# Four layers of a graph network on one core: where the adjacency transposes, the statistics and the additions of two layer boundaries stand in the order of work

## The chip, the cores and the metric

The kernel runs on one core of a Trainium2 chip. A core has five engines that run side by side, each with its own instruction stream: TensorE (PE in the profile) multiplies matrices and writes PSUM[...]; VectorE (DVE), ScalarE (ACT) and GpSimd (POOL) work element by element; SyncE (SP) here only issues the transfers between the chip's main memory and the core's SBUF. An engine takes its instructions in the order in which they stand in its stream. Engines wait for one another through semaphores, so an instruction whose input is late also holds up everything that stands behind it on its engine, whether or not that needed the late input.

The metric is the time of one execution on the device in microseconds (us). Of the kernel before there are three runs.

## The reference

The input x has 32 batches of 512 nodes with 128 features; adj is one 512 x 512 matrix with about one entry in eight above zero. There are four layers, each of the same outer form: normalise every node's features, cut at zero, apply a graph layer, add to x. Cut to what matters here:

```python
# each layer i:  h = max(layernorm(x), 0);  x = x + layer_i(h)

# layer 0: an attention matrix from adj's pattern and a list e of 256 values
m = adj > 0
idx = cumsum(m.reshape(-1)) - 1            # number of each entry above zero
A = softmax(where(m, e[0][idx], -9e15), axis=1)
out = (A * I) @ (h @ W[0]) + (A * (1 - I)) @ (h @ W[1]) + bias

# layer 1: two rounds of hops along adj, for A1 = A2 = adj
x1 = einsum('bnf,nw->bwf', h, adj)
x2 = 2 * einsum('bnf,nw->bwf', x1, adj) - h
out = relu(concat(h, x1, x2, x1, x2) @ Theta1 + bias)

# layer 2: weights adj * adj
features = relu(h @ psi_w + psi_b)
messages = einsum('nm,bnd->bmd', adj * adj, features)
out = relu(concat(messages, h) @ phi1_w + phi1_b) @ phi2_w + phi2_b

# layer 3: scores of h with itself, exp(8 tanh(s / 8)) times adj, divided by the row's sum
```

Because e has only 256 entries, the first 256 entries of adj above zero have a value of their own and all later ones share the last. The kernel finds the row and column of each of those 256 with counts and comparisons, and places their values in A by products of matrices that hold a single one in each row.

## The kernel before: what the change touches

The batches are taken in 16 groups q of two, and the groups in 8 pairs r. A product with the 512 x 512 matrix is done block by block with seven products in place of eight (Winograd's form of Strassen's scheme). GpSimd forms the differences of the right operand, named rt_g (layer 0), rt_h and rt_w (layer 1) and rt_feat (layer 2). The seven products are numbered by k; they use three PSUM banks a, c and d, which are written again as soon as VectorE or ScalarE has read them:

```python
    ORDER = ((1, "a", True), (6, "c", True), (5, "d", True), (7, "c", False), (2, "a", False),
             (4, "c", False), (3, "d", False))

    def products(name, form, left, right, evict):

        banks = {}
        for k, g, first in ORDER:
            if first:
                banks[g] = bank(f"p_{name}_{g}")
            form(banks[g], left[k], right[k], first)
            evict(k, banks[g])
            yield
```

```python
# layer 1 and layer 2 evict with this one: bank c holds k = 6, then 7, then 4
        def evict(k, p):
            p = p[:, :H]
            if k == 1:
                nc.scalar.copy(m1[0], p)
            elif k == 6:
                nc.vector.tensor_add(m1[1], p, m1[0])
            elif k == 7:
                nc.vector.tensor_add(m1[2], p, m1[0])
            ...
```

The preparation of layer 0 counts the entries of adj above zero (rc, incl, before), finds the 256 places (of_row, row_of, col_of, at_row, at_col, at_part) and fills att:

```python
    of_row = prep.tile([P, NT, NE], BF16, name="of_row")
    pb = bank("p_before")
    pg = [bank(f"p_row_{kk}") for kk in range(NK)]
    for t in range(NT):
        s = prep.tile([P, NE], F16, tag="lt", name=f"lt_{t}", bufs=4)
        nc.gpsimd.tensor_scalar(s, cols[:, :NE], incl[:, t : t + 1], None, OP.is_lt)
        nc.vector.scalar_tensor_tensor(of_row[:, t, :], cols[:, :NE], before[:, t : t + 1], s,
                                       OP.is_ge, OP.mult)
        for kk in range(NK):
            nc.tensor.matmul(pg[kk], of_row[:, t, blk(kk)], m[:, t, :], start=(t == 0), stop=(t == NT - 1))
    for kk in range(NK):
        for t in range(NT):
            nc.tensor.matmul(pb[:, kk : kk + 1], of_row[:, t, blk(kk)], befh[:, t : t + 1],
                             start=(t == 0), stop=(t == NT - 1))
# ... (parts of e in three lower-precision pieces, on GpSimd)
    us = [prep.tile([P, N], F32, tag="u", name=f"u_{t}", bufs=NT) for t in range(NT)]

    def entries(t):
        nc.scalar.mul(us[t], m[:, t, :], elastn)
        nc.gpsimd.tensor_add(att[:, t, :], us[t], att[:, t, :])

    entries(0)
    pt = [bank(f"p_adjT_{j}") for j in range(NT)]
    for t in range(NT):
        transpose_rows(pt, adj_s, t)
    for j in range(NT):
        nc.scalar.copy(adjT[:, j, :], pt[j])
    adjT_d = bounce.tile([N, N], F32, tag="adjT", name="adjT_d", bufs=1)
    nc.sync.dma_start(adjT_d.rearrange("(t p) w -> p t w", p=P), adjT)
    for kk in range(NK):
        s = prep.tile([P, N], F16, tag="scr", name=f"scr_r{kk}", bufs=2)
        nc.vector.tensor_scalar(s, pc, rows[:, kk : kk + 1], None, OP.is_le, OP.add,
                                accum_out=row_of[:, kk : kk + 1])
    ln = [stats_steps(q, powers=q < 2) for q in range(4)]
    go(ln[0])
    entries(1)
    go(ln[1])
# ... (scans, at_row, at_col, at_part, the first groups' h and its transposes)
    p = bank("p_qk_t")
    nc.tensor.transpose(p[:, blk(0)], qw, ident)
    nc.tensor.transpose(p[:, blk(1)], kw, ident)
    qkT = prep.tile([P, 2, D], F32, name="qkT")
    nc.scalar.copy(qkT, tiles(p)[:, :2, :])
    go(normal[1], 4)
    entries(2)
    entries(3)
    go(normal[1])
    bias(0)
```

`transpose_rows` makes the transpose of adj, which is written to main memory and read again much later, for layer 3:

```python
    def transpose_rows(banks, src, t):

        for j in range(NT):
            nc.tensor.transpose(banks[j][:, blk(t)], src[:, t, blk(j)], ident)
```

Up to the last pair but one of layer 0 the order on TensorE, VectorE, ScalarE and GpSimd is the order of the source. After that point a scheduler orders the instructions by its own estimates of their times:

```python
    for r in range(NQ // 2 - 1):
        round0(r)
    by_source.__exit__(None, None, None)

    next_layer = layer1(0)
    next(next_layer)
    waiting = [[next_layer, layer0_last()], [layer1(1)]]
    for r in range(2, NQ // 2):
        waiting += [[], [layer1(r)]]
    waiting[5].append(square())
    waiting[-1].append(layer2(0))
    waiting += [[layer2(q)] for q in range(1, NQ)]
    waiting += [[layer3(q)] for q in range(NQ)]
    active = []
    while waiting or active:
        if waiting:
            active += waiting.pop(0)
        if not waiting and len(active) == 2:
            active.reverse()
        active = [g for g in active if next(g, active) is not active]
```

Every generator in `active` is advanced one step in each turn of the loop; `yield` ends a step. The last pair of layer 0 and layer 1 before:

```python
    def layer0_last():
        round0(NQ // 2 - 1)
        go(own[NQ - 2])
        go(own[NQ - 1])
        yield

    # in layer1(r), the steps before this one: h[A] | turned(A), h[C] | first(A), turned(C) |
    # first(C), weighed(A) | weighed(C), right2 |
        for _ in products(f"l1_{r}", by_token, sums["adj"], right2, evict):
            pass
        p = bank(f"p_l1_{r}_e")
        own(p, 1, 1, True)
        done(p, u[2], 1, 1)
        if C == NQ - 1:
            yield
            yield
        ln_stats(A)
        ln_stats(C)
```

`turned` transposes h on VectorE (hb), sends it through main memory to get it feature by feature (hT), and forms rt_h; `first` forms x1T with `mixed`; `weighed` multiplies by Theta1 (p_w) and copies the result to w on ScalarE; the products named p_l then give the layer's output. `ln_stats` computes mean and variance of the new x with BATCH_NORM_STATS2 (bn), then the scale rs and the shift sh. In layer 0, `add` adds a partial sum to a block of x on GpSimd (line 751), and lines 745, 748 and 833 add products to the same blocks on VectorE. Layer 2 before:

```python
        feat = []
        for b in range(2):
            pf = projected(f"p_feat_{q}_{b}", (at(hT, b), psi))
            feat.append(late.tile([P, NT, D], F32, tag="hs", name=f"feat_{q}_{b}", bufs=6))
            nc.vector.tensor_add(feat[b], pf, spread(psib, NT))
            nc.scalar.activation(feat[b], feat[b], AF.Relu)
        yield
        right = right_blocks(lambda J, b: feat[b][:, 2 * J : 2 * J + 2, :], f"feat_{q}", [nc.gpsimd] * 4)
        if q % 2 == 0:
            msgs.append(quad_tile(f"msgT_{q}"))
        msgT = msgs[-1][:, q % 2, : 2 * N].rearrange("p (b w) -> p b w", b=2)
        for _ in mixed(f"msgT_{q}", sums["sq"], right, msgT):
            pass
        for b in range(2):
            for i in range(0, NT, 2):
                xi = xt[q][:, b, i : i + 2, :]
                tc.keep_in_program_order(nc.gpsimd.tensor_add(xi, xi, spread(phi2b, 2)))
        yield
```

## Time and profile before

| What | Before |
|---|---|
| median of three runs | 987.52 us (986.81 to 988.62) |
| span of the profiled execution | 989.5 us |
| instructions in it | 15113 |
| mean granted TensorE clock | 0.991 |
| ScalarE, first h of layer 0 | 19.25 us |
| TensorE, first product of layer 0 (p_l_a) | 39.12 us |
| TensorE, first product of layer 1 (p_x1T_a) | 192.96 us |
| TensorE, first product of layer 2 (p_msgT_a) | 467.90 us |
| main memory read and written | 44.17 MB and 40.89 MB |

The profile's page gives for one execution the time for which each engine was busy, the same in 40 equal slices of the span (a 9 means 90% or more), the groups of instructions that cost most, and the chain of work that ended last. Further views answer about a stretch of time: which instructions ran, how long an engine sat idle before one, and what released it (written as [idle <- releaser]). The granted clock is the share of its full rate at which TensorE was allowed to run; at 0.50 every product takes twice as long. A product is written as its output, then the inputs: `p_l_c<-rt_w,adj_s`.

### The profile page before, as it was taken

Reading aid. Unit: us, or ns where it says so; the run is one execution under the profiler, and the core shown is the slowest. Engines: PE = TensorE matmul, PEld = TensorE weight load, DVE = VectorE, ACT = ScalarE, POOL = GpSimd, SP = SyncE. Lnnn points to the kernel's source line nnn. Section 1 sums busy time; section 2 is a strip of 40 time slices with the busy share of each in tenths; the row PEclk is TensorE's granted clock in tenths of the full one; section 3 lists DMA queues with packets and bytes.
Section 4 is the critical chain, followed back from the end, with each engine's and each line's share of the span. In section 5 each row is a group of like instructions: output and inputs, shape, how many; then the busy total and the mean of one; then the engine's idle time right before and its main releaser. Section 6 shows DMA issues by size and latency. Waiting matters only on the chain.

```text
span 989.5 us, 15113 instructions
## 1 busy us (share of the span) xinstructions
PE 960.1 (97%) x5449; PEld 783.5 (79%) x5450; DVE 582.9 (59%) x1312; ACT 473.9 (48%) x1058; POOL 439.6 (44%) x482
## 2 busy tenths in 40 slices
PE   4999999899999999999799999999999999999998
PEld 2799999788988989889677777777667776777776
DVE  7778896636456445646367655656564444454444
ACT  4874555042332242376437454544665554445553
POOL 6686997923463532530623334444133322233322
PEclk9999999999999999999899999999999999999999
DMA  9145645223311311444133432232132121121111
GB/s 255 50 128 153 187 121 141 82 66 119 115 43 43 85 45 47 123 107 107 43 98 105 118 86 79 71 86 85 44 86 75 54 64 65 51 77 44 54 32 43
DMA packets 82330, 86.04 MB, mean 87 GB/s; under 512 B 6737, under 2 KB 72529, under 8 KB 82257
## 3 DMA queue, kind: packets, MB, share of 16 engines
q1 hardware_dynamic: 82256, 85.09, 30.7%
q8 instruction: 43, 0.70, 0.3%
q14 instruction: 31, 0.25, 0.1%
HBM read 44.17 MB, written 40.89 MB: 86 GB/s over the span
## 4 chain that ended last, share of the span: by engine, by line
PE 84%; POOL 6%; DVE 6%; ACT 2%; issue 1%; DMA 1%; SPq 0%; DVEq 0%; POOLq 0%; ACTq 0%
PE p_av L1025 12%; PE p_score L1010 11%; PE p_l_c L356 7%; PE p_w L405 5%; PE p_msgT_c L349 5%; PE p_l_a L356 5%; PE p_l_d L356 5%; PE p_x1T_c L349 4%; PE p_hv L405 3%; PE p_msgT_d L349 3%; PE p_feat L405 3%; PE p_qkh L997 3%; PE p_l L405 3%; PE p_msgT_a L349 3%; PE p_phi L980 3%; PE p_phi L981 3%
## 5 line engine op out<-in xcount | busy, mean ns | idle before, releaser
L231 ACT ACTIVATE h<-x,sh,rs 128x128 f32<-128x128 f32 x512 | 209.9, 484 | 81.9 <-PE p_x1T_d L349 33.2
L1015 POOL TENSOR_TENSOR ex<-ex,adjTx 128x512 f32<-128x512 f32 x64 | 83.1, 1300 | 206.4 <-ACT ex L1013 206.4
L1011 ACT ACTIVATE ex<-p_score 128x512 f32<-128x512 f32 x128 | 71.9, 587 | 124.6 <-issue 113.0
L1025 PEld LDWEIGHTS p_av<-qkh_hv,ex 128*128 128x128 f32 x1024 | 118.4, 191 | 9.4 <-issue 7.4
L1025 PE MATMUL p_av<-qkh_hv,ex 128*128 128x129 f32 x1024 | 120.1, 275 | 0.8 <-POOL ex L1015 0.8
L1010 PE MATMUL p_score<-qkh_hv,hT 128*128 128x512 f32 x256 | 115.2, 593 | 0.0
L265 DVE STREAM_TRANSPOSE hb_hT<-h 128x512 f32<-128x512 f32 x120 | 81.9, 697 | 35.6 <-ACT h L231 34.1
L1015 DVE TENSOR_TENSOR ex<-ex,adjTx 128x512 f32<-128x512 f32 x64 | 45.4, 709 | 82.2 <-ACT ex L1013 82.1
L203 DVE BATCH_NORM_STATS2 bn<-x 128x6 f32<-128x256 f32 x256 | 93.0, 418 | 1.1
L1010 PEld LDWEIGHTS p_score<-qkh_hv,hT 128*128 128x128 f32 x256 | 46.2, 190 | 46.5 <-issue 44.7
L1013 ACT ACTIVATE ex<-ex 128x512 f32<-128x512 f32 x128 | 76.6, 630 | 1.9
L330 POOL TENSOR_TENSOR rt_w<-w 128x512 f32<-128x512 f32 x16 | 20.3, 1269 | 108.2 <-ACT w L872 108.2
L330 POOL TENSOR_TENSOR rt_feat<-feat,feat 128x256 f32<-128x256 f32 x16 | 11.6, 728 | 127.3 <-ACT feat L964 127.3
L370 ACT COPY x1T<-p_x1T_a 128x256 f32<-128x256 f32 x16 | 5.9, 370 | 94.0 <-PE p_x1T_a L349 94.0
L405 PE MATMUL p_w<-th,x1T 128*128 128x128 f32 x256 | 49.5, 275 | 0.0
L405 PE MATMUL p_w<-th,hs 128*128 128x128 f32 x256 | 49.5, 275 | 0.0
L405 PEld LDWEIGHTS p_hv<-vw,hT 128*128 128x128 f32 x256 | 33.6, 192 | 15.3 <-issue 8.1
L975 POOL TENSOR_TENSOR x<-x,phi2b 128x256 f32<-128x256 f32 x64 | 44.5, 726 | 0.0
L982 ACT ACTIVATE msgT<-p_phi,phi1b 128x512 f32<-128x512 f32 x32 | 21.7, 678 | 41.0 <-PE p_phi L981 41.0
L405 PEld LDWEIGHTS p_w<-th,hs 128*128 128x128 f32 x256 | 40.1, 192 | 0.8
L964 ACT ACTIVATE feat<-feat 128x512 f32<-128x512 f32 x32 | 20.1, 629 | 42.2 <-DVE feat L963 42.2
L651 POOL TENSOR_TENSOR hd<-hT,adiag 128x512 f32<-128x512 f32 x32 | 39.8, 1272 | 1.2 <-ACT adiag L764 1.2
(229 smaller groups left out, 2085.3 us busy)
## 6 DMA issues: line engine op xcount, KB each, us to landing
d_hT<-hb_hT SPq DMA_DIRECT2D x240, 128.0 KB
hT<-d_hT SPq DMA_DIRECT2D x60, 512.0 KB
x<-in_x_dram SPq DMA_DIRECT2D x32, 256.0 KB
out_dram<-x SPq DMA_DIRECT2D x31, 256.0 KB
adj_s<-in_adj_dram SPq DMA_DIRECT2D x4, 256.0 KB
adjT_d<-adjT SPq DMA_DIRECT2D x1, 1024.0 KB
sq<-in_adj_dram SPq DMA_DIRECT2D x4, 256.0 KB
adjTx<-adjT_d SPq DMA_DIRECT2D x4, 256.0 KB
```

The source lines that it names most:

```text
L203: nc.vector.bn_stats(st[:, k].rearrange("p e s -> p (e s)"), xt[q][:, b, t : t + 2, :].rearrange("p t f -> p f t"))
L231: nc.scalar.activation(h[:, b, t, :], xt[q][:, b, t, :], AF.Relu, bias=shift[q][:, i : i + 1], scale=scale[q][:, i : i + 1])
L265: nc.vector.transpose(hb[:, :, b].rearrange("p j t r -> p t j r"), h[:, b].rearrange("p t (j c) -> p t j c", c=QR))
L349: nc.tensor.matmul(p[:, :H], b[:, k, :], a[:, k, :], start=(first and k == 0), stop=(k == 1), skip_group_check=True)
L356: nc.tensor.matmul(p[:, i * 2 * D : (i + 1) * 2 * D], a[:, k, blk(i)], b[:, k], start=(first and i == 0 and k == 0), stop=(k == 1), skip_g ...
L405: nc.tensor.matmul(p[:, blk(t)], hT(t), w, start=(i == 0), stop=(i == len(terms) - 1))
L975: tc.keep_in_program_order(nc.gpsimd.tensor_add(xi, xi, spread(phi2b, 2)))
L1010: nc.tensor.matmul(ps, hT[:, t, b, :], qkh, start=True, stop=True)
L1011: nc.scalar.activation(ex[:, t, :], ps, AF.Tanh, scale=1.0 / (8.0 * math.sqrt(D)))
L1013: nc.scalar.activation(ex[:, t, :], ex[:, t, :], AF.Exp, scale=8.0)
L1015: eng.tensor_mul(ex[:, t, :], ex[:, t, :], adjTx[0][:, t, :])
L1025: nc.tensor.matmul(po[:, i, : D + 1], ex[:, t, blk(i0 + i)], hv[:, t, :], start=(t == 0), stop=(t == NT - 1))
```

## The change

It is a change of order, save for 24 added products whose result nobody reads.

- The 16 transposes of adj and the four copies of their results stand right behind the load of adj, ahead of the counts. They stood behind the counts.
- `keep_busy(n)` issues n products of 128 x 512 into a bank that is not read, six after the counts and eighteen after p_before. They are meant to keep TensorE from standing still.
- The four comparisons lt go from GpSimd to VectorE; elastn, u and the additions to att are placed differently among the first statistics.
- The last pair of layer 0 is put into the part that keeps the order of the source, with the first two steps of layer 1 woven in by hand; layer 1's second pair starts one turn earlier; the statistics of groups 14 and 15 come a turn later.
- In layer 1 a `yield` stands between the last addition and the statistics, so these belong to the next turn.
- In layer 2 the differences rt_feat are formed in the same turn as feat, not in the next.

```diff
--- before.py
+++ after.py
@@ -461,6 +461,20 @@
     att = square_tile("att")
     for t in range(NT):
         nc.gpsimd.tensor_scalar(att[:, t, :], m[:, t, :], -1.0, -NEG, OP.add, OP.mult)
+    pt = [bank(f"p_adjT_{j}") for j in range(NT)]
+    for t in range(NT):
+        transpose_rows(pt, adj_s, t)
+    for j in range(NT):
+        nc.scalar.copy(adjT[:, j, :], pt[j])
+    adjT_d = bounce.tile([N, N], F32, tag="adjT", name="adjT_d", bufs=1)
+    nc.sync.dma_start(adjT_d.rearrange("(t p) w -> p t w", p=P), adjT)
+
+    def keep_busy(n):
+
+        p = bank("p_idle")
+        for _ in range(n):
+            nc.tensor.matmul(p, upto[:, 0, blk(0)], upto[:, 0, :], start=True, stop=True)
+
 
     pi = bank("p_incl")
     for t in range(NT):
@@ -477,13 +491,14 @@
     nc.vector.tensor_sub(before, incl, rc)
     befh = prep.tile([P, NT], BF16, name="befh")
     nc.vector.tensor_scalar(befh, before, float(NE), None, OP.min)
+    keep_busy(6)
 
     of_row = prep.tile([P, NT, NE], BF16, name="of_row")
     pb = bank("p_before")
     pg = [bank(f"p_row_{kk}") for kk in range(NK)]
     for t in range(NT):
-        s = prep.tile([P, NE], F16, tag="lt", name=f"lt_{t}", bufs=4)
-        nc.gpsimd.tensor_scalar(s, cols[:, :NE], incl[:, t : t + 1], None, OP.is_lt)
+        s = prep.tile([P, NE], F16, tag="lt", name=f"lt_{t}", bufs=2)
+        nc.vector.tensor_scalar(s, cols[:, :NE], incl[:, t : t + 1], None, OP.is_lt)
         nc.vector.scalar_tensor_tensor(of_row[:, t, :], cols[:, :NE], before[:, t : t + 1], s,
                                        OP.is_ge, OP.mult)
         for kk in range(NK):
@@ -492,13 +507,12 @@
         for t in range(NT):
             nc.tensor.matmul(pb[:, kk : kk + 1], of_row[:, t, blk(kk)], befh[:, t : t + 1],
                              start=(t == 0), stop=(t == NT - 1))
+    keep_busy(18)
     row_of = prep.tile([P, NK], F32, name="row_of")
     col_of = prep.tile([P, NK], F32, name="col_of")
     at_row = prep.tile([P, NK, N], BF16, name="at_row")
     at_col = prep.tile([P, NK, N], BF16, name="at_col")
     at_part = prep.tile([P, 3, NK, N], BF16, name="at_part")
-    elastn = prep.tile([P, 1], F32, name="elastn")
-    nc.gpsimd.tensor_scalar(elastn, elast, -1.0, None, OP.mult)
 
     ecoln = prep.tile([P, NK], F32, name="ecoln")
     nc.gpsimd.tensor_scalar(ecoln, ecol, -1.0, None, OP.mult)
@@ -512,26 +526,25 @@
         if i < 2:
             nc.gpsimd.tensor_sub(ecoln, ecoln, part)
         parts.append(part)
+    elastn = prep.tile([P, 1], F32, name="elastn")
+    nc.gpsimd.tensor_scalar(elastn, elast, -1.0, None, OP.mult)
     us = [prep.tile([P, N], F32, tag="u", name=f"u_{t}", bufs=NT) for t in range(NT)]
 
+    def value(t):
+        nc.scalar.mul(us[t], m[:, t, :], elastn)
+
     def entries(t):
-        nc.scalar.mul(us[t], m[:, t, :], elastn)
         nc.gpsimd.tensor_add(att[:, t, :], us[t], att[:, t, :])
 
-    entries(0)
-    pt = [bank(f"p_adjT_{j}") for j in range(NT)]
-    for t in range(NT):
-        transpose_rows(pt, adj_s, t)
-    for j in range(NT):
-        nc.scalar.copy(adjT[:, j, :], pt[j])
-    adjT_d = bounce.tile([N, N], F32, tag="adjT", name="adjT_d", bufs=1)
-    nc.sync.dma_start(adjT_d.rearrange("(t p) w -> p t w", p=P), adjT)
+    value(0)
+    value(1)
     for kk in range(NK):
         s = prep.tile([P, N], F16, tag="scr", name=f"scr_r{kk}", bufs=2)
         nc.vector.tensor_scalar(s, pc, rows[:, kk : kk + 1], None, OP.is_le, OP.add,
                                 accum_out=row_of[:, kk : kk + 1])
     ln = [stats_steps(q, powers=q < 2) for q in range(4)]
     go(ln[0])
+    entries(0)
     entries(1)
     go(ln[1])
     bk = prep.tile([P, NK], F32, name="bk")
@@ -557,7 +570,9 @@
     nc.tensor.transpose(p[:, blk(1)], kw, ident)
     qkT = prep.tile([P, 2, D], F32, name="qkT")
     nc.scalar.copy(qkT, tiles(p)[:, :2, :])
-    go(normal[1], 4)
+    go(normal[1], 2)
+    value(2)
+    value(3)
     entries(2)
     entries(3)
     go(normal[1])
@@ -812,6 +827,8 @@
                 go(own_a)
             elif i == 3:
                 add(1, 1, 2)
+                if not more:
+                    next(next_layer)
                 if C + 4 < NQ:
                     normalise(C + 4)
                 if r >= 3:
@@ -838,11 +855,11 @@
         if r + NQ // 4 < NQ // 2:
             loads(r + NQ // 4)
 
-    def layer0_last():
-        round0(NQ // 2 - 1)
+    def layer0_stats():
+
+        yield
         go(own[NQ - 2])
         go(own[NQ - 1])
-        yield
 
     x1 = []
 
@@ -935,6 +952,7 @@
         p = bank(f"p_l1_{r}_e")
         own(p, 1, 1, True)
         done(p, u[2], 1, 1)
+        yield
         if C == NQ - 1:
             yield
             yield
@@ -962,8 +980,8 @@
             feat.append(late.tile([P, NT, D], F32, tag="hs", name=f"feat_{q}_{b}", bufs=6))
             nc.vector.tensor_add(feat[b], pf, spread(psib, NT))
             nc.scalar.activation(feat[b], feat[b], AF.Relu)
-        yield
         right = right_blocks(lambda J, b: feat[b][:, 2 * J : 2 * J + 2, :], f"feat_{q}", [nc.gpsimd] * 4)
+        yield
         if q % 2 == 0:
             msgs.append(quad_tile(f"msgT_{q}"))
         msgT = msgs[-1][:, q % 2, : 2 * N].rearrange("p (b w) -> p b w", b=2)
@@ -1049,13 +1067,13 @@
             nc.gpsimd.tensor_copy(sq[:, i, :], s)
         yield from sum_steps(sq, "sq")
 
-    for r in range(NQ // 2 - 1):
+    next_layer = layer1(0)
+    for r in range(NQ // 2):
+        if r == NQ // 2 - 1:
+            next(next_layer)
         round0(r)
     by_source.__exit__(None, None, None)
-
-    next_layer = layer1(0)
-    next(next_layer)
-    waiting = [[next_layer, layer0_last()], [layer1(1)]]
+    waiting = [[next_layer, layer1(1), layer0_stats()]]
     for r in range(2, NQ // 2):
         waiting += [[], [layer1(r)]]
     waiting[5].append(square())
```

How the instructions stand after it, engine by engine, is known from the two built programs. On TensorE layer 1's p_w products, which stood between the x1T products of the pair ahead, now stand behind all seven of them. On VectorE the first x1T eviction of a pair (line 372) stands ahead of three of the four last statistics, and was behind them. On GpSimd at the first boundary the order was hd, rt_h, hs and the additions to x in turns, and is now four hd, three additions, twelve rt_h. At the second boundary it was rt_w, then rt_feat, and is now rt_feat, then rt_w.

More of the change, by code (lines that the diff above doesn't have):

```diff
@@ L964, in layer2 @@
             nc.scalar.activation(feat[b], feat[b], AF.Relu)
+        right = right_blocks(lambda J, b: feat[b][:, 2 * J : 2 * J + 2, :], f"feat_{q}", [nc.gpsimd] * 4)
         yield
-        right = right_blocks(lambda J, b: feat[b][:, 2 * J : 2 * J + 2, :], f"feat_{q}", [nc.gpsimd] * 4)
         if q % 2 == 0:
```

## The prediction

> **What bounds the kernel now.** I read first the page's busy times and the slices, to see whether one engine carries the span.
>
> ```profile
> PE 960.1 (97%) x5449; PEld 783.5 (79%) x5450; DVE 582.9 (59%) x1312; ACT 473.9 (48%) x1058; POOL 439.6 (44%) x482
> PE   4999999899999999999799999999999999999998
> ```
>
> TensorE (PE) is busy for 960.1 of 989.5 us, and its work does not get less. So a change that only reorders can win two things: the 29.4 us in which PE stands still, and the time in which it works at half clock. The slices that are not 9 (first, eighth, twentieth, last) say where to look. Next I read the waits of PE, summed by what it waited for (us in total, times, longest).
>
> ```profile
> PE p_incl L468 <- DVE rch L458: 8.3, 1, 8.3
> PE p_msgT_c L349 <- POOL rt_feat L330: 5.4, 1, 5.4
> PE p_x1T_c L349 <- DVE rs L217: 5.0, 7, 2.6
> PE p_hT L249 <- ACT h L231: 3.6, 1, 3.6
> ```
>
> The first is the load of adj and the first row counts, which nothing in the diff shortens. The other three are the change's three targets: layer 1 to layer 2 (5.4), layer 0 to layer 1 and inside layer 1 (5.0 in seven pieces), and the preparation (3.6). Then the stretches of 1 us around them (columns: PE, PEld, DVE, ACT, POOL busy; then the granted clock, DMA share, GB/s):
>
> ```profile
> 26.00:27.00 1.00, 1.00 (x3) 0.30 (x2) 0.16 (x1) 1.00 (x4) 0.91 (x1) 0.50 1.02 367
> 200.00:201.00 1.00, 1.00 (x4) 0.73 (x4) 0.59 (x2) 0.00 (x0) 0.00 (x0) 0.50 0.00 0
> 480.00:481.00 1.00, 1.00 (x3) 0.74 (x3) 0.00 (x0) 0.00 (x0) 0.00 (x0) 0.50 0.00 0
> ```
>
> PE is full there, but at clock 0.50. Finer stretches put the half clock at 20.6 to 27.4, 198.1 to 201.5 and 474.6 to 481.4 us: each follows a gap. A gap thus costs twice. Last I read the order in time at the two layer boundaries:
>
> ```profile
> 189.25 0.73 POOL L330 TENSOR_TENSOR rt_h<-h 128x256 f32<-128x256 f32 x1
> 194.83 1.26 POOL L751 TENSOR_TENSOR x<-x,u_l 128x512 f32<-128x512 f32 x1
> 196.13 0.69 DVE L833 TENSOR_TENSOR x<-p_l_e,x 128x512 f32<-128x512 f32 x1 [2.62 <-POOL x L751]
> 197.74 0.41 DVE L372 TENSOR_TENSOR x1T<-p_x1T_c,x1T 128x256 f32<-128x256 f32 x1
> 198.29 2.05 PE L349 MATMUL p_x1T_c<-adj_s,rt_h 128*128 128x256 f32 x4 [2.57 <-DVE rs L217]
> ...
> 468.99 1.27 POOL L330 TENSOR_TENSOR rt_w<-w 128x512 f32<-128x512 f32 x1 [18.57 <-ACT w L872]
> 474.01 0.72 POOL L330 TENSOR_TENSOR rt_feat<-feat,feat 128x256 f32<-128x256 f32 x1
> 476.15 2.08 PE L349 MATMUL p_msgT_c<-sums_sq,rt_feat 128*128 128x256 f32 x4 [5.41 <-POOL rt_feat L330]
> 484.93 1.89 PE L356 MATMUL p_l_a<-w,adj_s 128*128 128x256 f32 x8
> ```
>
> At 190 us GpSimd works on layer 1's differences (rt_h) while layer 0's last addition to x waits behind them. VectorE stands in order at that x (2.62 us), and behind it lies the eviction L372 that frees PE's bank. At 469 us GpSimd takes four rt_w first; rt_feat, which PE needs next, had its input at 466.0 us and starts at 474.0.
>
> [...] half clock lasted 6.8, 3.4 and 6.8 us, once after a gap of only 2.57 us. [...] of_row took 0.70, 0.69, 0.69 us beside GpSimd's lt and 0.48 us after it.
>
> **The change, part by part.** Times are on the clock of before, each part alone.
>
> *Preparation.* The 16 transposes of adj leave 14.2 to 16.2 us and run as adj arrives; their four ScalarE copies (2.05 us) leave 15.9 to 17.9. The four lt (3.65 us on GpSimd, 9.0 to 12.7) go to VectorE, at about 0.2 us each (a 128x512 comparison of the same types takes 0.35). Four pairs of lt and of_row at some 0.7 us end at 12.2 instead of 13.1. The first statistics then end near 15.0, and GpSimd, free of lt and of the att addition (1.27 us) that stood ahead, ends scale and shift near 17.6 instead of 19.2. ScalarE's first h starts 1.6 us earlier. The second pair's scale and shift gain less, because both att additions (2.5 us) now stand ahead: near 22.7 instead of 23.3. ScalarE then does two h, two u, six h, and reaches its first exponential near 27.3 instead of 28.06. The unread products (6, then 18, at 0.215 us each at full clock: 1.3 and 3.9 us) fill PE's idle time; none is waited for, except that a cold PE makes the first six last 2.6 us and could delay p_row, whose reader VectorE comes only near 16.4. If they keep the clock, the 32 products of p_first and p_val run at 1.72 us a row from the start, and the 1.4 us (0.91, 0.20, 0.29) that ScalarE lost in waits for least shrink. ScalarE's row of exponentials, scalings, g copies and table load then sets the start of layer 0: 0.75 plus about 1.0 gives 1.8 us.
>
> *Layer 0 to layer 1.* GpSimd's order now is hd, the three additions, then rt_h. The rt_g end at 179.2, four hd at 1.27 at 184.2, the additions near 188.0 (the third waits for L739). L833 follows p_l_e at 192.6, no longer 196.1. VectorE then still has some 1.5 us of statistics ahead of L372, so that runs near 195.3 to 196.2, and PE, which has x1T_d done at 195.0, waits 0.6 to 1.3 us[...]. Before, these seven x1T products took from 192.96 to 203.4, 10.4 us; at 0.86 us each they need 6.05. Of the 4.4 us and the 0.31 before p_l_c, about 3.5 are won.
>
> *Inside layer 1.* Six gaps remain (5.0 less 2.6: 2.4 us; one of 0.78, five near 0.3). The order on VectorE now puts L372 ahead of three of the statistics (1.1 us). But PE has also lost the p_w products that stood between, so c7 waits 0.15 us where it waited 0.3. I count 1.2 us.
>
> *Layer 1 to layer 2.* rt_feat is now ahead of rt_w on GpSimd, and PE does all seven msgT products in a row. rt_feat can start at 466.1, its third operation, which c needs, ends near 468.2; PE is at 468.8. The rt_w follow, 469.0 to 474.1, and p_l_c needs the second of them at 477.5. PE from msgT_a (467.90) to p_l_a (484.93) took 17.0 us; its work is 7 x 0.86 + 16 x 0.112 = 7.8. That gives 9.2; I count 9.0.
>
> Sum: 1.8 + 3.5 + 1.2 + 9.0 = 15.5, and 987.5 - 15.5 = 972.0 us. Layer 3 and the last 3.7 us of idle PE are untouched.
>
> **Rivals.** *Preparation goes cold or slower.* For it: the h transposes come one in 0.39 us, and PE was at half clock through just such a stretch; then rows take 3.4 us for a while. This leaves 0 to 1 us of the 1.8: 973 to 974. [...] *VectorE becomes the bound at the first boundary.* It now carries the transposes hb of two pairs and all statistics between 185 and 196 with GpSimd beside it; an L218 there took 0.91 us instead of 0.2. L372 at 197.5 would make the gap 2.5 us and cold again: 975. *The second boundary only moves its wait.* ScalarE was full from 458 to 474 us with h of layer 2, and the copies of w and msgT stand between them; if L370 slips by 2 us, PE waits that long: 974. Against: its place is the same as before. *Everything is found*: preparation follows PE rather than ScalarE (3.0), the boundary gives 4.4, layer 1 2.4, then 968.5, still short of 967.8, which 2% would need.
>
> **Range and chances.** Most of the sum rests on the last part, whose arithmetic leaves little room. The parts before may each miss by 1 us, and a new gap with its cold clock costs 3 to 5. I give 967.5 to 978. Faster by over 2% needs 19.8 us, all parts at their limit: 0.07. Slower by over 2%: 0.01.
>
> **What would show it.** PE's waits should no longer list rt_feat, the longest p_x1T_c wait should be under 1.5 us, and p_hT's under 1.5. Half clock should be gone near 196 and 475. L833 should not wait for POOL. PE's busy time should grow by about 5 us of unread products. A page with rt_feat's wait still there, or a new row above 2 us, makes the prediction wrong; so does layer 0 starting later than 39 us.

## Result, and the profile after

The changed kernel takes 974.49 us (median of 4 runs, 973.98 to 974.86) where the kernel before, run beside it, took 988.07: a ratio of 0.9859, 95% interval 0.9837 to 0.988. Run again beside the kernel before, it gave 974.23 and 0.9854 (0.9837 to 0.987). That is 1.4% less, within 2%; 972.0 had been predicted, with a range of 967.5 to 978.

The page of the changed kernel, busy times and slices:

```profile
PE 959.0 (99%) x5474; PEld 781.9 (80%) x5474; DVE 581.0 (60%) x1316; ACT 474.6 (49%) x1058; POOL 436.5 (45%) x478
PE   7999999999999999999999999999999999999998
PEclk9999999999999999999999999999999999999999
```

TensorE's idle time fell from 29.4 to 13.7 us. The dents in the eighth and twentieth slice are gone, only the first and last are left. Its waits (us in total, times, longest):

```profile
PE p_adjT L444 <- DMA adj_s<-in_adj_dram: 4.7, 2, 3.8
PE p_x1T_c L349 <- DVE x1T L372: 2.5, 7, 0.4
PE p_msgT_c L349 <- DVE msgT L372: 0.6, 1, 0.6
```

rt_feat (5.4 us) and the transposes of h (3.6) no longer stand in the list, and p_x1T_c's longest wait went from 2.6 to 0.4. The stretches of 1 us that answer to the three shown of before (last columns: granted clock, DMA share, GB/s):

```profile
26.00:27.00 1.00, 1.00 (x6) 0.49 (x5) 0.63 (x2) 1.00 (x4) 1.00 (x2) 1.00 0.98 365
194.00:195.00 1.00, 1.00 (x5) 0.90 (x6) 1.00 (x3) 0.00 (x0) 1.00 (x3) 1.00 0.04 13
463.00:464.00 1.00, 1.00 (x6) 0.80 (x5) 0.19 (x1) 1.00 (x4) 0.92 (x2) 1.00 0.00 0
```

TensorE is as full as before, but at clock 1.00, and starts five or six products in a us where it started three or four. The order in time at the two boundaries:

```profile
182.64 3.76 POOL L766 TENSOR_TENSOR x<-x,u_l 128x512 f32<-128x512 f32 x3
191.28 0.69 DVE L850 TENSOR_TENSOR x<-p_l_e,x 128x512 f32<-128x512 f32 x1
193.43 0.40 DVE L372 TENSOR_TENSOR x1T<-p_x1T_c,x1T 128x256 f32<-128x256 f32 x1
193.98 1.10 PE L349 MATMUL p_x1T_c<-adj_s,rt_h 128*128 128x256 f32 x4 [0.22 <-DVE x1T L372]
...
458.92 0.73 POOL L330 TENSOR_TENSOR rt_feat<-feat,feat 128x256 f32<-128x256 f32 x1 [15.47 <-ACT feat L982]
461.63 1.03 PE L349 MATMUL p_msgT_c<-sums_sq,rt_feat 128*128 128x256 f32 x4
461.79 1.27 POOL L330 TENSOR_TENSOR rt_w<-w 128x512 f32<-128x512 f32 x1
468.60 1.89 PE L356 MATMUL p_l_a<-w,adj_s 128*128 128x256 f32 x8
```

GpSimd's three additions to x are done at 186.4, before layer 1's differences; VectorE's last addition (L850, L833 before) waits for nothing; TensorE waits 0.22 us for L372, not 2.57 (the list of before put these waits down to L217, which ran just behind L372). Below, rt_feat comes before rt_w, and TensorE goes from p_msgT_a (460.76) to p_l_a (468.60) in 7.8 us, not 17.0.

### The profile page after: what moved, and what is told of

It reads as the page before. It is cut to its first block, busy times and chain, and to the rows that moved or that the text cites. A ratio compares the mean times of both kernels' runs of the same rounds, so it can differ in the third digit from the quotient of the medians.

```text
span 972.7 us, 15180 instructions
## 1 busy us (share of the span) xinstructions
PE 959.0 (99%) x5474; PEld 781.9 (80%) x5474; DVE 581.0 (60%) x1316; ACT 474.6 (49%) x1058; POOL 436.5 (45%) x478
## 4 chain that ended last, share of the span: by engine, by line
PE 91%; DVE 4%; ACT 2%; DMA 2%; SPq 1%; issue 0%; POOL 0%; DVEq 0%; ACTq 0%
PE p_av L1043 12%; PE p_score L1028 11%; PE p_l_c L356 9%; PE p_l_a L356 6%; PE p_l_d L356 6%; PE p_w L405 5%; PE p_msgT_c L349 4%; PE p_x1T_c L349 4%; PE p_feat L405 3%; PE p_hv L405 3%; PE p_msgT_d L349 3%; PE p_msgT_a L349 3%; PE p_qkh L1015 3%; PE p_l L405 3%; PE p_g L405 3%; PE p_phi L998 3%
## 5 line engine op out<-in xcount | busy, mean ns | idle before, releaser
L265 DVE STREAM_TRANSPOSE hb_hT<-h 128x512 f32<-128x512 f32 x120 | 81.7, 697 | 33.4 <-ACT h L231 33.1
L370 ACT COPY x1T<-p_x1T_a 128x256 f32<-128x256 f32 x16 | 5.9, 370 | 84.3 <-PE p_x1T_a L349 84.3
L1048 DVE SCALAR_TENSOR_TENSOR x<-p_av,rsum,x 128x128 f32<-128x128 f32 x128 | 39.1, 347 | 1.9
```

The lines of the kernel that those rows point to most:

```text
L265: nc.vector.transpose(hb[:, :, b].rearrange("p j t r -> p t j r"), h[:, b].rearrange("p t (j c) -> p t j c", c=QR))
```

## The experiments

I cut each trace at the first start of a few products. "rch" is VectorE's cast of the row counts, which comes right after the last part of adj has landed. p_adiag is a product early in layer 0, p_phi the first product of layer 2 that follows its messages. Durations in us, worked out from those starts:

| stage | before | prep_alone | boundary_alone | feat_alone | after |
|---|---|---|---|---|---|
| start to rch | 8.1 | 8.2 | 6.8 | 7.6 | 8.0 |
| rch to p_adiag | 34.8 | 33.4 | 34.6 | 34.0 | 33.5 |
| p_adiag to p_x1T_a (layer 0) | 150.1 | 150.1 | 149.5 | 150.1 | 149.5 |
| p_x1T_a to p_l_a of w (first boundary) | 29.9 | 30.0 | 25.7 | 30.0 | 25.7 |
| to p_msgT_a (layer 1) | 245.0 | 245.0 | 244.1 | 245.0 | 244.0 |
| to p_phi (second boundary) | 32.7 | 33.1 | 32.0 | 23.5 | 23.5 |
| to the end | 489.0 | 488.5 | 488.7 | 489.3 | 488.4 |

The three large moves, at the two boundaries and inside layer 1, each come with one part and stay away where it is missing. Smaller ones, 0.8 us from rch to p_adiag (feat_alone beside before) and 0.4 to 0.7 at the second boundary, come without an edit there; each column is one run.

### feat_alone: only rt_feat a step earlier

```
-        yield
         right = right_blocks(lambda J, b: feat[b][:, 2 * J : 2 * J + 2, :], f"feat_{q}", [nc.gpsimd] * 4)
+        yield
```

> The kernel before with only one part of the change: layer 2's four differences rt_feat are formed one step of the generator earlier, so that GpSimd takes them up before the differences rt_w. Theory: this is the largest single term. In the profile the stretch from the first product of p_msgT_0_a to the first product of p_l_a with w shrinks from 17.0 to about 7.8 us (it holds 7.8 us of products), the half clock near 475 us is gone, and the time falls by 7 to 9.5 us, to 978 to 981. Rival (the wait only moves, to ScalarE's feat or to rt_w): the stretch still holds a gap of 2 us or more and the time falls by less than 5 us. Second theory tested here, on the runs of the kernel before that stand beside this one: its times differ from run to run [...] a longer run of the kernel before shows a lower mean granted clock, about 0.4% of clock for each 4 us, and this kernel's runs spread over less than the 3.9 us that the kernel before has shown.

Measured: 980.24 us, ratio 0.9909 (0.9891 to 0.9927), which is 9.0 us (7.2 to 10.8) of 988.9. p_msgT_a to p_l_a took 7.8 us (466.62 to 474.45), and nothing took the wait's place. Waits of TensorE in this kernel:

```profile
PE p_x1T_c L349 <- DVE rs L217: 5.0, 7, 2.6
PE p_msgT_c L349 <- DVE msgT L372: 1.2, 2, 1.0
```

The other wait of before is untouched, rt_feat is gone, and p_msgT_c waits 1.0 us at most. The first theory holds. The second one, that the scatter goes with the half clock, holds in part. Its four runs spread over 3.7 us, no less than before's, all at a granted clock of 0.996 or 0.997. But over all 47 runs of the kernel before in this study (986.48 to 991.13), those with a mean granted clock of 0.991 took 989.81 us on average (19 runs) and those with 0.993 took 988.07 (20 runs). The difference, 1.74 us, is close to what one more stretch at half clock as long as the shortest of before (198.09 to 201.50, 3.41 us) would cost (half of it, 1.71 us, by my estimate). Eight runs at 0.995 took 988.65 and don't go on with the series, so the clock is at most a part of the scatter.

### boundary_alone: only the last pair in source order, with layer 0's statistics later

```
-    def layer0_last():
-        round0(NQ // 2 - 1)
+    def layer0_stats():
+        yield
         go(own[NQ - 2])
...
+            if r == NQ // 2 - 1:  next(next_layer)
             round0(r)
```

Layer 1's second step inside the last pair and the earlier start of its second pair belong to this edit too.

> The kernel before with only the part of the change at the boundary of layers 0 and 1: the last pair of layer 0 is issued in source order, layer 1's first step is put into it, and layer 0's last statistics come two steps later. Theory: the seven products p_x1T_a to p_x1T_d of the first quad take 6.5 us from start to end instead of 10.4, the half clock near 200 us is gone, the wait of the last products of layer 0 for rt falls by 0.3 us, and the time falls by 3.5 to 4.5 us, to 983 to 984. Rival (the statistics put off return as waits of VectorE inside layer 1): the stretch of the first quad is shorter, but the lead at the first product of layer 1's p_l_a is under 2 us and the time falls by less than 2 us.

Measured: 983.62 us, ratio 0.9945 (0.9928 to 0.9961): 5.4 us (3.9 to 7.1), more than expected. The seven x1T products of the first pair of groups (a quad in the expectations) do take 6.5 us. What comes on top is in the table: 0.6 in the last pair, 4.2 at the boundary, and 0.9 inside layer 1, which I had put down to another part. Waits of TensorE:

```profile
PE p_msgT_c L349 <- POOL rt_feat L330: 5.4, 1, 5.4
PE p_x1T_c L349 <- DVE rs L217: 1.6, 5, 0.3
```

p_x1T_c's waits are 1.6 us in five pieces, and 0.2 in one more that is put down to L372: less even than the 2.5 in seven of the changed kernel.

### stats0_undone: the boundary's part split

```
     def layer0_stats():
-        yield
         go(own[NQ - 2])
         go(own[NQ - 1])
+        yield
```

> The changed kernel with layer 0's last statistics issued in the step right after the last pair, as in the kernel before, while the last pair stays in source order with layer 1's first step inside it. It splits the 5.3 us that the boundary's part gave alone. Theory (the source order of the last pair does it: the additions to x and the differences of the first quad come at their place on GpSimd, and x1T's first eviction is no longer behind them): the stretch from p_x1T_a to the first p_l_a with w stays within 0.6 us of the changed kernel's 25.7 and the time within 0.7 us of 974.5. Rival (the statistics, eight times 0.4 us on VectorE, were what stood ahead of x1T's evictions and the transposes): the stretch goes back by 2 us or more towards the 29.9 us of the kernel before, and the time rises by 2 us or more, with half clock near 197 us again.

Measured: 974.51 us; the first boundary takes 25.7 us (190.8 to 216.5) as in the changed kernel. So putting off layer 0's statistics is worth nothing here. The trace shows how little the edit moved: VectorE's order up to the first L372 (193.18) is that of the changed kernel, and the statistics put back come behind it. What is left of that part, the source order with layer 1's first two steps inside the last pair and its second pair a turn earlier, does it; I didn't run these apart.

### stats_undone: layer 1's statistics back in their old step

```
         done(p, u[2], 1, 1)
-        yield
```

> The changed kernel with layer 1's statistics issued again in the same step as the last products (the one yield taken out). The prediction gave this part 1.2 us. Theory: VectorE then takes three 0.4-us statistics ahead of the eviction L372 in seven quads, each such wait of p_x1T_c grows by 0.15 us or more, and the stretch from layer 1's first p_l_a with w to the first p_msgT_a, 244.1 us, becomes 245.0; the time rises by 0.8 to 1.2 us, to about 975.5. Rival (the boundary's part moved the same waits already: the kernel with that part alone had 244.2 us there): the stretch stays within 0.3 us of 244.1 and the time within 0.4 us of 974.5.

Measured: 974.34 us, layer 1's stretch 244.1, beside 244.0 in the changed kernel. The rival holds. Waits of TensorE in this kernel:

```profile
PE p_x1T_c L349 <- DVE rs L217: 1.6, 5, 0.3
PE p_msgT_c L349 <- DVE msgT L372: 1.0, 1, 1.0
```

With the yield they are 2.5 and 0.6 us, without it 1.6 and 1.0, to which come 0.2 for one wait more: 3.1 against 2.8. The yield wins none. It does bring L372 forward: counted from the start of the p_x1T_c product that L372 reads, L372 runs 1.75 us later (235.01) in the changed kernel and 2.75 us later (234.61) without the yield. But TensorE is done with what stands before its wait 1.90 us after that start instead of 2.98, because a p_x1T_a product and two p_w products have moved behind it. The wait is 0.41 us with the yield and 0.33 without.

### prep_alone: only the preparation

The whole of the diff ahead of the score rows (the products p_first and p_val, which fill att row by row), and nothing after it.

> The kernel before with the whole of the change's preparation (transposes of adj back in front, unread products, the row masks on VectorE, ScalarE's order of value and h) and nothing else. Theory: p_adiag's first product starts 1.3 to 1.5 us earlier than at 42.88 us, no half clock at 20 to 27 us, and the time falls by 1.3 to 1.8 us, to about 986.0, since after the preparation TensorE has nearly no slack. Rival (the lead is lost again at the first boundary of layers, where GpSimd and not TensorE sets the pace): the lead at p_adiag is there but the time changes by less than 0.5 us.

Measured: 989.57 us over 12 runs beside 988.89 over 15: ratio 1.0001 (0.9993 to 1.001). No gain, although rch to p_adiag took 33.4 us. The half clock at 20 to 27 us was not gone either: 20.4 to 23.8 ran at 0.50 in spite of the unread products. The second boundary may show where part of the lead went. The kernel's order in time there:

```profile
468.42 1.13 PE L349 MATMUL p_msgT_a<-sq,feat 128*128 128x256 f32 x4 [0.67 <-ACT msgT L370]
472.81 0.72 POOL L330 TENSOR_TENSOR rt_feat<-feat,feat 128x256 f32<-128x256 f32 x1
474.94 2.07 PE L349 MATMUL p_msgT_c<-sums_sq,rt_feat 128*128 128x256 f32 x4 [5.39 <-POOL rt_feat L330]
```

The gap is the 5.4 us of before, but the half clock now holds from 470.9 to 481.2, 10.3 us where before had 6.8, and the stage takes 33.1 us instead of 32.7. That is one run, and 0.4 us; where the rest went is not shown.

### prep_undone: everything but the preparation

The changed kernel with before's text ahead of the score rows.

> The changed kernel with the preparation of the kernel before put back (transposes of adj late, no unread products, row masks on GpSimd, old order of value and h); the boundary, the statistics and rt_feat as changed. The preparation alone moved the time by nothing that could be measured (ratio 1.0001, 0.9993 to 1.001), although in the traces its stretch from the cast of the row counts to p_adiag was 33.4 us where the kernels with the old preparation had 33.9, 34.6 and 34.8. Theory A (the lead of about 1 us is real, and was given back in the kernel before at its boundaries[...]): without those boundaries the lead counts, and this kernel takes 0.7 to 1.5 us more than the changed one, 975.2 to 976.0. Theory B (the start of the program jitters by more than the lead, and the preparation is worth nothing): the time is 974.5 within 0.4 us.

Measured: 974.62 us (974.35 to 975.19), ratio 0.9864 (0.9844 to 0.9883). That is 0.1 to 0.4 above the medians of the changed kernel, 974.49 and 974.23. The time is the one that theory B names. In the trace, rch to p_adiag is 34.2 us and p_adiag to the end 931.0, against 33.5 and 931.2: from rch on, the changed preparation leads by 0.5 us.

### no_busy: without the unread products

```
-    keep_busy(6)
...
-    keep_busy(18)
```

> The changed kernel without its 24 unread products in the preparation (6 and 18 products of 128x512 into a bank that nothing reads), nothing else taken out. Theory (the unread products buy the clock): TensorE is at half speed for some 7 us between 18 and 29 us, the score rows take longer, p_adiag starts 0.8 to 2 us later than the 41.5 us of the changed kernel, and the time rises by that, to about 975.5. Rival (the order of the work was what counted, and ScalarE bounds this stretch anyhow): the half clock comes back but p_adiag starts within 0.4 us of 41.5 and the time stays within 0.5 us of 974.5.

Measured: 974.72 us (973.59 to 975.33), and rch to p_adiag 33.3 us: the rival holds. (p_adiag itself came at 40.4 us, 1.2 before that of the changed kernel, since rch came 1.0 earlier.) Stretches of 1 us of this kernel (columns as above):

```profile
18.00:19.00 1.00, 1.00 (x3) 0.41 (x3) 0.96 (x2) 1.00 (x4) 0.97 (x1) 0.50 1.17 291
20.00:21.00 1.00, 1.00 (x5) 0.66 (x5) 1.00 (x4) 0.90 (x3) 1.00 (x1) 0.50 1.17 289
24.00:25.00 1.00, 1.00 (x6) 0.49 (x5) 0.71 (x3) 1.00 (x4) 1.00 (x1) 1.00 0.45 74
```

TensorE was at half clock from 15.5 to 22.4 us and, counted from rch, layer 0 started no later for it: in these us others set the pace.

### after_again: the changed kernel unedited

> The changed kernel once more, nothing edited, beside the kernel before, for the scatter of its times and of its start. So far four runs of it gave 973.98 to 974.86; with the old preparation (all else changed) 974.35 to 975.19; without the unread products 973.59 to 975.33; the two better preparations 971.56 to 973.31 and 972.08 to 973.38. Theory (what the preparation of the change gains, about 1 us from the cast of the row counts to p_adiag in the traces, is real but less than the scatter of the loads in front of it, 1.4 us): the median is 974.0 to 974.6, so 0 to 0.6 us under the old preparation's, and the cast of the row counts lies anywhere from 6.8 to 8.2 us while p_adiag follows it by 33.3 to 33.5 us. Rival (the preparation's lead counts in full): 973.6 or less.

Measured: 974.23 us (973.78 to 974.7), rch at 8.0 and p_adiag 33.4 after it. In this trace the clock was at half from 20.9 to 24.3 in spite of the unread products. Of the six traces with the change's preparation and its unread products, five have such a stretch of 3.4 us there (prep_alone, stats_undone, stats0_undone, finish_pool and this one); only the changed kernel's first trace has none. rch to p_adiag is 33.3 to 33.5 us in all six.

### finish_pool: an addition of layer 1 given to GpSimd

```
-            nc.vector.scalar_tensor_tensor(x, y, 0.0, x, OP.max, OP.add)
+            nc.gpsimd.tensor_scalar(y, y, 0.0, None, OP.max)     # block (1, 1) of six pairs
+            nc.gpsimd.tensor_add(x, x, y)
```

> The changed kernel with one of layer 1's four final additions per pair (relu of u added to x, 0.67 us on VectorE, in front of the eviction L372 that TensorE waits for) done by GpSimd in two steps of about 1.27 us, in six of eight pairs. Theory: VectorE reaches L372 0.2 us earlier in six quads, the wait of p_x1T_c (2.5 us in all) falls by about 1.2 us, and the time by about 1 us, to 973.5. Rival (GpSimd's own additions and differences come later by 2.5 us a pair and TensorE waits for rt_w or hs in their place): the time stays or rises by up to 3 us.

Measured: 991.6 us, 17 more than the changed kernel and slower than the kernel before (ratio 1.0032, 1.0019 to 1.0045). Neither theory had this size. The worst of six places, in order of time:

```profile
314.48 1.27 POOL L925 TENSOR_TENSOR x<-x,u_l 128x512 f32<-128x512 f32 x1
315.79 0.77 DVE L203 BATCH_NORM_STATS2 bn<-x 128x6 f32<-128x256 f32 x2 [8.13 <-POOL x L925]
317.23 2.04 PE L349 MATMUL p_x1T_c<-adj_s,rt_h 128*128 128x256 f32 x4 [7.47 <-DVE sh L218]
```

GpSimd did the squares of adj first and ended the addition at 315.75, where its input had been there since 306.55. VectorE stood in order at the statistics of that x (8.13 us), and the eviction of p_x1T_c that TensorE needed next stood behind them. Such waits of TensorE sum to 15.1 us in six pieces, and the clock was at half for 6.8 us in and behind this one. It is the first boundary's old fault made anew.

### prep2, prep3, prep4: three other preparations

All on the changed kernel; prep3 and prep4 keep the first projection of prep2 ahead of the score rows. The cores of the edits:

```
 prep2   +        nc.tensor.matmul(ph, identh, m[:, t, :], start=True, stop=False)   # m by TensorE
         -    value(0..3), entries(0..3)                    # ScalarE's m * elastn, GpSimd's additions
         +    go(ln[0])  ahead of the row counts;  go(project[0])  ahead of the score rows
 prep3   +    first statistics ahead as in prep2;  value(0..3) early;
              entries(0..3) after the second statistics;  no product of m
 prep4   +    rows 2, 3 of m by TensorE;  value(0, 1), entries(0, 1) right after the first statistics,
              which come ahead of of_row;  bias(0) after the first scaled row;  keep_busy(10) for (18)
```

> An attempt at a better preparation, on the changed kernel: m is added to the first-entry scores by TensorE (one more 128x512 bf16 product per row tile against a bf16 identity, so that ScalarE's four products m*elastn and GpSimd's four additions to att go), the statistics of the first quad come ahead of the two row counts on VectorE, and the first projection is issued ahead of the score rows. Theory (ScalarE and GpSimd bound this stretch): the first h starts 1 to 1.4 us earlier than 17.7, the first exponential about 25 to 26 us instead of 27.7, p_adiag 1 to 2 us earlier than 41.5, and the time falls by 1 to 2 us, to about 973. Rival (TensorE bounds it once the transposes of h have begun, and four more products cost it 1.2 us): p_adiag moves by less than 0.5 us.

Measured: 972.55 us (971.56 to 973.31), ratio 0.984 (0.9823 to 0.9858). h began at 16.0, the first exponential at 25.7, and rch to p_adiag took 31.7 us. The theory holds. From then on TensorE has little slack: its waits from 17 us to p_adiag sum to 0.9 us.

> A second attempt at the preparation, on the changed kernel. The trace of the first attempt (972.55) shows TensorE as the bound from its score rows on (21.86 to 29.63 us, 7.8 us with the four extra products of m), while ScalarE waited 6.3 us for the first shift and GpSimd 4.9 us before bias. So m*elastn and the additions to att stay where they were made, on ScalarE and GpSimd, but all four of each go into those idle stretches, and no product is added to TensorE; the statistics of the first quad still come ahead of the row counts, and the first projection ahead of the score rows. Theory: the score rows take 6.5 us again, p_adiag starts about 1.2 us earlier than in the first attempt counted from the cast of the row counts (30.5 us after it instead of 31.7; 33.5 in the changed kernel), and the time is 971 to 972. Rival (the additions to att end too late for the first softmax row, or ScalarE's products delay the first h): p_adiag is not earlier than in the first attempt and the time is 972.5 or more.

Measured: 976.29 us, 1.8 more than the changed kernel. The rival holds, for a reason it didn't name. The order in time:

```profile
18.50 5.04 POOL L537 TENSOR_TENSOR att<-u,att 128x512 f32<-128x512 f32 x4
20.08 1.06 DVE L577 TENSOR_SCALAR at_row<-cols,row_of 128x512 bf16<-128x512 f16 x1
21.06 1.35 DVE L578 TENSOR_SCALAR at_col<-cols,col_of 128x512 bf16<-128x512 f16 x1
25.01 0.38 PE L593 MATMUL p_first<-at_col,at_row 128*128 128x512 bf16 x1 [2.15 <-DVE at_col L578]
```

Beside GpSimd's additions a mask took 1.06 to 1.35 us; in prep2, without them, each of the four took 0.35. Together 5.1 us instead of 1.4, and TensorE waits for the last of them. The masks end 1.27 to 1.28 us apart, about the length of one addition (1.26). What holds a mask up beside an addition is not shown here.

> A third attempt at the preparation, on the changed kernel, drawn from the traces of the first two. In the second attempt (976.29) the four row and column masks at_row and at_col took 1.06 to 1.35 us each on VectorE while GpSimd's additions to att ran beside them (0.35 us each in the first attempt and in the changed kernel), which cost about 3.9 us. Here only rows 0 and 1 of att are added by GpSimd, ahead of the second quad's shift and so ahead of the masks; rows 2 and 3 take m by one more product each on TensorE; the first quad's statistics come ahead of the row masks of of_row, the bias of x comes after the first scaled row, and 10 unread products stand in place of the 18. Theory: the masks take 0.35 us again, the first h starts at about 14 us, the first score product about 1 us earlier than 21.9, the score rows take 7.1 us instead of 7.8, and p_adiag starts about 30.2 us after the cast of the row counts instead of the first attempt's 31.7: the time is 970.5 to 971.5. Rival (x of the first quad has not landed when VectorE comes to its statistics, or the additions to att now slow the scans and of_row): p_adiag is not earlier than in the first attempt and the time is 972.5 or more.

Measured: 972.42 us (972.08 to 973.38), ratio 0.983 (0.9816 to 0.9843). The masks took 0.35 us again, h began at 12.7, and rch to p_adiag took 31.1 us instead of the 30.2 expected, so neither theory nor rival has it whole. In time it isn't told apart from prep2. Both beat the changed kernel by about 2 us: their nine runs lie between 971.56 and 973.38, the changed kernel's eight between 973.78 and 974.86, though the intervals of the ratios overlap (0.9816 to 0.9858 beside 0.9837 to 0.988).

## Why the prediction was right, and where not

The time was within the range, 2.5 us above 972.0. By its terms:

- **Layer 1 to layer 2, 9.0.** Right: 9.0 us (7.2 to 10.8) alone, 7.8 us of products from p_msgT_a to p_l_a as worked out. Both costs of the gap, the wait and the half clock behind it, went together. The rival of a wait moved to ScalarE's L370 fell: 0.6 us is left, for VectorE's L372.
- **Layer 0 to layer 1, 3.5.** The mechanism was right: GpSimd's order, L833 standing at x, L372 behind it. The whole ran ahead by 2.0 us (p_x1T_a at 191.00 instead of 192.96). With that added, x was done at 188.4 (predicted 188.0), L850 ran at 193.3 (192.6) and L372 at 195.4 (195.3 to 196.2). The wait was 0.22 us instead of 0.6 to 1.3, because "x1T_d done at 195.0" was too early: in before that product starts at 194.69 and fills TensorE until 195.7. The size was short: "of the 4.4 us and the 0.31 before p_l_c, about 3.5 are won", and the traces show 4.2 at the boundary and 0.6 in the last pair, all that was to be had. The statistics put off, which the prediction didn't separate, did nothing of this.
- **Inside layer 1, 1.2.** Wrong step. Layer 1 did get shorter by 0.9 to 1.0 us, but through the boundary's part, which took its waits there from 2.4 to 1.6 us; the yield named for it gives nothing. "c7 waits 0.15 us where it waited 0.3" (c7 is product 7, in bank c) measured 0.41: the three statistics (1.1 us) did go behind L372, but TensorE came to c7 1.1 us earlier too, more than was allowed for, and VectorE still had the last addition to x (L921, 0.67 us) ahead of L372.
- **Preparation, 1.8.** The failed step is "ScalarE's row of exponentials [...] sets the start of layer 0: 0.75 plus about 1.0". The first h did start early (17.71, predicted 17.6). But the second pair's shift, "near 22.7 instead of 23.3", ended at 23.3 as before, behind GpSimd's two additions to att, and ScalarE waited for it:

```profile
17.64 2.49 POOL L537 TENSOR_TENSOR att<-u,att 128x512 f32<-128x512 f32 x2
23.37 0.88 ACT L231 ACTIVATE h<-x,sh,rs 128x128 f32<-128x128 f32 x2 [1.18 <-POOL sh L213]
```

So the first exponential came at 27.68 instead of 27.3: a lead of 0.4 us, and counted from rch of 0.3 to 0.5 over all traces, not 0.75. The other term is ScalarE's waits for least, the row's smallest value that VectorE hands it. They did shrink by 1.0 us between the two profiled runs. But with the old preparation alone they range from 1.4 to 0.4 us, in step with the clock:

| traces | half clock ends, us after rch | ScalarE's waits for least | rch to p_adiag |
|---|---|---|---|
| before | 19.3 | 1.4 | 34.8 |
| boundary_alone | 19.0 | 1.2 | 34.6 |
| prep_undone | 18.1 | 0.7 | 34.2 |
| feat_alone | 16.6 | 0.4 | 34.0 |
| seven with the new preparation | 15.1 to 16.3, one without | 0.4 | 33.3 to 33.5 |

The first four traces have the same preparation. That the clock makes their difference is argued from this order, not tested. On average the new one leads by 1.0 us at p_adiag (33.4 beside 34.4), and of that the times show 0.1 to 0.4 in one comparison and none in the other. In front of rch, adj's landing scatters by 1.4 us from run to run (6.8 to 8.2), so this needs more runs than these; what became of the rest stays open. That a lead in the preparation does reach the end is shown by prep2: 1.7 us of it gave 1.7 to 1.9 us.
- **The base.** I subtracted from 987.5, the median of three runs. The 47 later runs of the same kernel average 988.9. The parts that work, 5.4 and 9.0, taken from 988.9 give 974.5. So the sum was 1.1 too large, and the base 1.4 too low; the two errors added up to the 2.5. (Side by side with the kernel before, the changed one was 13.6 and 13.5 us faster, less than that sum but within the intervals.)
- **The trace alone misleads here.** Between the two profiled runs the span fell by 16.8 us, more than predicted, because the profiled run of before, 991.6 us, was above all 47 of the others.
- **What would show it.** Five of the six signs came as said. "PE's busy time should grow by about 5 us" didn't: it went from 960.1 to 959.0. The unread products do take 6.4 us, but half clock had counted as busy (the three stretches of before at 0.50 show PE at 1.00), and most of that is gone. One sign of being wrong, "a new row above 2 us", did come by its letter: p_adjT's 4.7 us (and p_x1T_c's 2.5, the old row under another name). p_adjT waits for the load of adj, as p_incl did for 8.3 us before; the sign was badly chosen.

## What to carry to other kernels

An engine that works in order passes a late input on to everything behind it, however unrelated (8.13 us in finish_pool): look not at what TensorE waits for but at what stands in front of that on its engine, and move the work there, or the work in front of its input, before lightening any load. Judge a part by undoing it alone in the final kernel: here layer 1's later statistics, layer 0's later statistics and the unread products were each worth nothing that could be measured. And take the base from enough runs: three gave 987.5 us where 47 average 988.9.

## What the runs showed of the hardware that was not expected

- In each of two traces, all edges of half clock that were read lie a whole number of times 3.413 us apart: in before at 20.60, 27.42, 198.09, 201.50, 474.57 and 481.40, which is 2, 50, 1, 80 and 2 times; in finish_pool at 20.03, 23.44, 313.58 and 320.40, which is 1, 85 and 2 times. Counted from the start of the span the two series do not lie on each other: less whole multiples of 3.413, the first edge leaves 0.1 us in before and 3.0 in finish_pool. One and the same gap (5.4 us at the second boundary) was followed by 6.8 us of half clock in before and by 10.3 in prep_alone.
- The time from the last product to the fall of the clock was not the same from gap to gap. In prep_alone TensorE stopped at 469.55 and the clock fell at 470.9, 1.4 us later; in before it stopped at 195.7 and the clock fell at 198.1, 2.4 us later, and again at 470.7 and 474.6, 3.8 us.
- Half clock in the preparation cost nothing that the traces show where it ended up to 16.3 us after rch (33.3 to 33.5 us to p_adiag with 6.8, 3.4 and 0 us of it); with the old preparation the traces in which it ended later were also slower, by up to 0.8 us (the table above). At the second boundary of before three groups of four products at half clock took 1.9 to 2.1 us each, the next two, at full clock, 1.03. In these traces the clock counted where TensorE, or an engine that waited for it, set the pace.
